# A quarter of a depthwise convolution's taps by ScalarE and adding DMAs, and its layernorm moved into the first MLP matmul

## The chip, the cores and the metric

The kernel runs on one core of a Trainium2 chip. The metric is the device time of one execution in microseconds. Before the change it is 3346.98 us (median of three runs, 3346.12 to 3347.55); the profiled execution spans 3346.6 us with a mean granted TensorE clock of 0.996. All data are float32.

## The reference

The input is eight images of 384 channels and 32 x 32 pixels, that is 1024 tokens of 384 channels. Two layers follow each other.

The first is a transformer block. A layernorm (ln1), q, k and v of 8 heads of 48 channels, softmax attention, a projection (proj) added to the input, a second layernorm (ln2), a linear layer to 1536 channels (fc1) with GELU, a linear layer back to 384 (fc2), added again.

The second is a ConvNeXt block on the first one's output:

```python
y = conv_general_dilated(x, dw_w, padding=((3,3),(3,3)), feature_group_count=384)  # 7x7, one filter per channel
y = layernorm over channels (y + dw_b)                # ln3
y = gelu(y @ w1 + b1)                                 # 384 -> 1536
gx = sqrt(sum over pixels of y**2)
y = gamma * (y * gx / (mean(gx) + eps)) + beta + y    # global response norm
out = x + y @ w2 + b2                                 # 1536 -> 384
```

The depthwise convolution has 49 taps per channel. Nothing is summed over channels in it, so it is not a matmul.

## The kernel before, in words

Channels lie on the 128 partitions: an image is three tiles of 128 channels (index `ct`) by 1024 tokens, and most work goes by halves of 512 tokens. TensorE does the matmuls; fc2, the 384 -> 1536 product of the second block and the 1536 -> 384 product use hand-made fast block multiplications, which trade matmuls for additions on VectorE.

The images overlap by one. In the loop over `b` in `main`, the first layer of image b is computed, and between its parts the second layer of image b-1. In order of TensorE: q and k (`qk`), attention (scores `s`, exp on ScalarE into `p`, products `o`), proj for the first token half, the rest of the attention, fc1 for the first half (`gelu_half`; after its fourth tile `rest` does proj for the second half), fc1 for the second half, fc2 (`by_thirds`), `grn_up` of image b-1 (rows named h), the v matmuls of image b+1, `grn_down` of image b-1 (rows named o_p). The last image goes another way (`mlp_by_halves`, `grn_up_straight`), and its own convolution, in two bands of rows written over the space of the attention's weights (rows named wqkv), has to run before the end.

The convolution (`convolution`, L880) is one instruction per tap and channel tile on VectorE: `acc = window * tap + acc` (L897), 128 x 1024, on a padded copy of the image (`pad`). The 147 instructions of an image are spread over the time of TensorE from the end of `grn_up` to the end of fc1, so that they fill VectorE between its other duties. `Flow` does this spreading: it keeps a planner's clock, which advances by `U` = 0.857 us with each matmul that is written out (`flow.pe`), and side work is a generator that yields the time until its next step is due. A paced chain keeps its own due times. So all queues are in an order fixed when the program is built. `flow.finish` writes out what is left of a chain at once. The second argument of `start_conv` is the time between two taps (1.8 us in the steady images, 1.6 for image 0's convolution, 1.5 for image 6's), the third says for how many rounds of three they are 2.43 us apart.

A layernorm (`layernorm`, L393) takes the sum over channels, subtracts the mean, sums the squares and scales. The sum over partitions is a matmul with a matrix of ones (`token_sums`, L367). Unfolded this is one 128 x 128 matmul of 512 columns per half and sum (L374). Folded, a DMA issued by GpSimd first adds one half of the partitions onto the other (L382), and 64 x 64 matmuls (L388) run side by side in the array. The folded way needs a wait for that DMA, for which the planner leaves 3.4 us. ln1 and the first half of ln2 are folded, the second half of ln2 and ln3 are not. `abreast` runs the two halves of a layernorm together.

ln3 of image b-1 is started by `next_norms`, which `mlp` calls just before fc2: it finishes the convolution's chain, and spawns ln3 followed by `block_differences` (four subtractions that `grn_up` needs). ln1 of image b+1 comes 50 us or more after this.

The attention normalises its products by sums that travel through three small DMAs on SyncE's queue (`average`, L547: sums, back, r), before the multiplication at L579 that proj waits for.

DMAs issued by GpSimd (rows marked POOLq) go out in order of its queue. In fc1 these are the two `difference` DMAs (fc_e, L708) that prepare fc2, in fc2 and `grn_down` the `adding` DMAs (L786).

Of the kernel before, what the change touches and what calls it, by code (L numbers as in the profile page):

```python
# [51 lines left out]
P = 128  # L52
# [12 lines left out]
CM = 2  # L65
NC = HT // CM
U = 0.857
SCALE = HD ** -0.5
EPS0, EPS1, GRN_EPS = 1e-5, 1e-6, 1e-6
SUM_LOW, SUM_HIGH = 1e-25, 1e25  # L70
# [80 lines left out]
def block_kernel(  # L151
# [429 lines left out]
    def attention(b, xt, qT, kT, last_tile, first):  # L581


        sums = two.tile([P, 2 * NP * 8], F32, tag="sums", name=f"sums_{b}")
        outs, chains, ps, backs = {}, {}, {}, ({}, {})

        def scores(qh, m, t):
            s = ps_s.tile([P, 2, NH], F32, tag="s", name=f"s_{b}_{qh}_{m}_{t}")
            for j in range(2):
                for i in range(2):  # L590
                    k0 = t * P + 64 * i
                    nc.tensor.matmul(  # L592
                        out=s[64 * i : 64 * i + 64, j, :],
                        lhsT=kT[64 * j : 64 * j + HD, m, k0 : k0 + 64],
                        rhs=qT[64 * j : 64 * j + HD, m, half(qh)],
                        start=True,
                        stop=True,
                    )
            flow.pe(U)
            p = three.tile([P, 2, NH], F32, tag="p", name=f"p_{b}_{qh}_{m}_{t}")  # L600
            nc.scalar.activation(p, s, AF.Exp)  # L601
            return p

        def product(qh, m, t, p):
            if t == 0:
                for i in range(2):
                    outs[i] = o_tile(f"o_{b}_{qh}_{m}_{i}")
            for i in range(2):
                keys = slice(64 * i, 64 * i + 64)
                for j in range(2):  # L610
                    at = (2 * m + j) * VW
                    nc.tensor.matmul(  # L612
                        out=outs[i][64 * j : 64 * j + 64, :],
                        lhsT=v[keys, t, at : at + 64],
                        rhs=p[keys, j, :],
                        start=(t == 0),
                        stop=(t == KT - 1),
                    )
            flow.pe(U)
            if t == KT - 1:  # L620
                chains[qh, m] = flow.spawn(average(b, qh, m, dict(outs), sums, backs[qh]))

        steps = [(qh, m, t) for qh in range(2) for m in ORDER for t in range(KT)]
        ln_table()
        ln = None
        for n in range(len(steps) + 2):
            if n == 2:
                last_tile()
            if n < len(steps):
                ps[n] = scores(*steps[n])  # L630
            if n >= 2:
                product(*steps[n - 2], ps.pop(n - 2))
            if n - 2 == len(steps) // 2 + 6:
                for chain in first:
                    flow.finish(chain)
                xn = one.tile([P, CT, N], F32, tag="xn", name=f"xn2_{b}")
                for m in (NP - 1, *range(CT)):
                    flow.finish(chains[0, m])
                proj(b, xt, 0)
                slow = 1.4 if b in (1, B - 1) else 1.0  # L640
                ln = layernorm(xt, xn, 0, eps0, "g2", f"ln2_{b}", False, spaced=True, slow=slow, fold="columns")
                ln = flow.spawn(ln)
# [75 lines left out]
    def mlp(b, xt, xn, weights, tag, ln, rest, before_fc2):  # L718

        hid = one.tile([P, HT * N], F32, tag="big", name=f"hid_{b}").rearrange("p (m n) -> p m n", m=HT)  # L720
        e = [three.tile([P, 2, NH], F32, tag="p", name=f"fc2_e_{b}_{i}") for i in range(2)]
        wa = f"fc1_{tag}"
        flow.finish(ln)
        for m in range(HT):
            gelu_half(hid, m, 0, xn, weights, wa, f"fc1_{b}")
            if m == 3 and rest:
                rest()
                slow = 1.2 if b == 1 else 1.0
                ln = flow.spawn(layernorm(xt, xn, 1, eps0, "g2", f"ln2_{b}", True, slow=slow))
        flow.finish(ln)  # L730
# [146 lines left out]
        nc.sync.dma_start(out=kept.rearrange("(c p) n -> p c n", p=P), in_=xt)  # L877
        return kept

    def convolution(acc, us, slow=0, y0=0, y1=H, ready=tuple(range(CT))):  # L880

        done = [0] * CT
        ct, n = None, 0
        while min(done) < KS * KS:
            left = [c for c in ready if done[c] < KS * KS]
            ct = min([c for c in left if c != ct] or left, key=lambda c: done[c])
            i = done[ct]
            dy, dx = divmod(i, KS)  # L890
            window = pad[:, ct, dy + y0 : dy + y1, dx : dx + W]
            dst = image(acc[:, ct, :])[:, y0:y1, :]
            tap = col("dww", ct * KS * KS + i)
            if i == 0:
                nc.vector.tensor_scalar(dst, window, tap, col("dwb", ct), ALU.mult, ALU.add)
            else:
                nc.vector.scalar_tensor_tensor(dst, window, tap, dst, ALU.mult, ALU.add)  # L897
            done[ct] += 1
            n += 1
            yield 2.43 if n <= CT * slow else us  # L900

    def block_differences(acc):

# [76 lines left out]
    def grn_down_straight(b, y, kept, weights, tag, index, todo):  # L980
# [5 lines left out]
        def load():  # L986
            if len(res) < len(todo):
                r, part = todo[len(res)]
                t = three.tile([P, NH], F32, tag="res", name=f"res_{b}_{r}_{part.start}")[:, : part.stop - part.start]
                nc.sync.dma_start(out=t, in_=kept[r * P : (r + 1) * P, part])  # L990
                res.append(t)

# [162 lines left out]
    def prepare(weights, aside):  # L1155
# [23 lines left out]
            return parts  # L1179

        def spare(name):
            return three.tile([P, NH], F32, tag="res", name=name)

        def sub(dst, x, y):
            nc.vector.tensor_tensor(dst, x, y, ALU.subtract)
# [119 lines left out]
    def main():  # L1305
# [41 lines left out]
        state = {"xn": xn, "conv": None, "acc": None, "norm1": None, "norm3": None}  # L1347
        kept = {}

        def start_conv(b, us, slow=0):  # L1350
            state["acc"] = one.tile([P, CT, N], F32, tag="acc", name=f"acc_{b}")
            state["conv"] = flow.spawn(convolution(state["acc"], us, slow), paced=True)

        def next_norms(b, ln=None):
# [28 lines left out]

        def last_convolution(h, ct, ln=None):
            if ct < 0:
                next_norms(B - 1, ln)
                return
            ready[h].append(ct)
            if ct == 0:
# [6 lines left out]
        for b in range(B):  # L1396
# [4 lines left out]
            qT, kT, last_tile = qk(b, state["xn"])  # L1401
            ln2, rest, xn = attention(b, xt, qT, kT, last_tile, (folding, aside) if b == 0 else ())
            if b < B - 1:
                mlp(b, xt, xn, weights, b, ln2, rest, lambda: next_norms(b))
# [58 lines left out]
    def exact_path():  # L1463

        load_wqkv(nc.scalar, nc.scalar)
        with tc.For_i(0, B) as b:
# [11 lines left out]
            mlp("x", xt, xn, weights, "x", ln, None, None)  # L1478
# [111 lines left out]
```

## Time and profile before

| | value |
|---|---|
| time, median of three | 3346.98 us |
| TensorE busy | 3303.6 us, 99% |
| VectorE busy | 2550.6 us, 76% |
| ScalarE busy | 1421.0 us, 42% |
| GpSimd busy | 208.1 us, 6% |
| DMA, mean | 84 GB/s; GpSimd's queue 77.08 MB, 11.9% of 16 engines' span |
| convolution taps, 128 x 1024 | 1008 of 1276 ns |
| period of a steady image | 404.3 us (a row of fc1 at 1346.57 and at 1750.83) |

A row of the costliest groups gives line, engine and operation, what is written and read, shapes and count, then the busy time in us and the mean of one in ns, then the idle time of the engine just before, and what ended it. In the order of time, a row merges equal instructions that follow each other: start, duration, engine, line, and how many. A float32 matmul shows as two records; ends of matmuls are modelled, so the distance of two starts tells what one takes. In a list of DMA issues the last number is the median time from issue to landing.

### The profile page before, as it was taken

What the parts mean: (1) busy time and instruction counts of PE and PEld (TensorE: products, weight loads), DVE (VectorE), ACT (ScalarE), POOL (GpSimd) and SP (SyncE); (2) the same over time, 40 slices, a digit from 0 to 9 for tenths busy, and PEclk for the clock granted to TensorE, in tenths of its full rate; (3) what the DMA queues carried; (4) which work ended last, traced back from release to release, by engine and by line L of the source; (5) the groups of instructions that cost most, each with busy time, mean ns of one, the idle gap of its engine ahead of it and who ended that gap; (6) DMA issues with size and microseconds to landing.
All of it is one profiled execution on the core that took longest, in us unless ns stands there. A gap on an engine that the chain in (4) does not pass through costs nothing.

```text
span 3346.6 us, 37477 instructions
## 1 busy us (share of the span) xinstructions
PE 3303.6 (99%) x14282; PEld 1416.7 (42%) x14282; DVE 2550.6 (76%) x3133; ACT 1421.0 (42%) x1884; POOL 208.1 (6%) x243
## 2 busy tenths in 40 slices
PE   8999999999999999999999999999999999999999
PEld 4344434443344433444334443444434444334455
DVE  4344788887877878779797796967888779989950
ACT  3442453444534354352552625426254353522641
POOL 2121000100000000100001000010000110000000
PEclk9999999999999999999999999999999999999999
DMA  5336102642125410445005350062501633023231
GB/s 185 111 105 148 52 20 57 158 102 63 25 70 146 115 47 20 105 122 135 20 16 131 96 140 17 17 157 80 128 18 37 170 83 95 20 56 90 62 98 50
DMA packets 151243, 281.59 MB, mean 84 GB/s; under 512 B 35216, under 2 KB 41232, under 8 KB 150672
## 3 DMA queue, kind: packets, MB, share of 16 engines
q1 hardware_dynamic: 114704, 201.32, 19.6%
q0 software_dynamic: 36064, 77.08, 11.9%
q8 instruction: 115, 1.88, 0.2%
q10 hardware_dynamic: 288, 0.71, 0.1%
q14 instruction: 72, 0.59, 0.1%
HBM read 181.52 MB, written 33.82 MB: 64 GB/s over the span
## 4 chain that ended last, share of the span: by engine, by line
PE 87%; DVE 10%; DMA 2%; issue 1%; ACT 0%; SPq 0%; POOL 0%; DVEq 0%; POOLq 0%
PE o L612 12%; PE s L592 12%; PE fc L345 12%; PE h L352 10%; PE fc_p L352 10%; PE o_p L352 9%; PE qk L332 6%; DVE wqkv L897 4%; PE v L521 4%; PE o L1000 4%; PE proj L535 3%; DVE acc L897 3%; PE h_last L1044 1%; PE qk_last L345 1%; PE ln_var L374 1%
## 5 line engine op out<-in xcount | busy, mean ns | idle before, releaser
L897 DVE SCALAR_TENSOR_TENSOR acc<-pad,vec,acc 128x1024 f32<-128x1024 f32 x1008 | 1230.6, 1276 | 0.0
L601 ACT ACTIVATE p<-s 128x1024 f32<-128x1024 f32 x512 | 523.6, 1024 | 380.6 <-PE s L592 378.4
L592 PE MATMUL s<-qk 48*64 48x512 f32 x4096 | 544.0, 592 | 1.6 <-ACT qk L495 1.5
L612 PE MATMUL o<-p,v 64*64 64x512 f32 x4096 | 538.9, 590 | 0.0
L345 PE MATMUL fc<-xn,fc 128*128 128x512 f32 x1152 | 500.4, 593 | 0.0
L345 PEld LDWEIGHTS fc<-xn,fc 128*128 128x128 f32 x1152 | 218.2, 190 | 278.2 <-issue 268.2
L352 PE MATMUL fc_p<-hid,fc 128*128 128x512 f32 x728 | 318.1, 592 | 0.0
L364 ACT ACTIVATE hid<-fc,bfc_f 128x512 f32<-128x512 f32 x192 | 130.9, 687 | 357.5 <-PE fc L345 357.4
L612 PEld LDWEIGHTS o<-p,v 64*64 64x64 f32 x4096 | 158.6, 133 | 284.6 <-issue 278.1
L592 PEld LDWEIGHTS s<-qk 48*64 48x64 f32 x4096 | 155.5, 133 | 286.0 <-issue 264.3
L945 DVE TENSOR_TENSOR y<-h,y 128x512 f32<-128x512 f32 x288 | 197.2, 690 | 97.8 <-PE h L352 87.3
L352 PE MATMUL o_p<-y,w 128*128 128x512 f32 x624 | 270.9, 592 | 0.0
L352 PEld LDWEIGHTS fc_p<-hid,fc 128*128 128x128 f32 x728 | 138.2, 190 | 174.4 <-issue 170.4
L332 PE MATMUL qk<-xn,wqkv 128*128 128x512 f32 x480 | 207.4, 592 | 0.0
L352 PE MATMUL h<-acc,w_A 128*128 128x512 f32 x432 | 206.4, 596 | 0.0
L897 DVE SCALAR_TENSOR_TENSOR wqkv<-pad,vec,wqkv 128x416 f32<-128x416 f32 (+1 forms) x288 | 193.7, 749 | 0.6
L352 PEld LDWEIGHTS o_p<-y,w 128*128 128x128 f32 x624 | 118.0, 190 | 148.7 <-issue 133.5
L553 DVE TENSOR_TENSOR attn<-o,attn 128x512 f32<-128x512 f32 x64 | 44.1, 689 | 147.2 <-ACT attn L551 147.2
L495 ACT ACTIVATE qk<-qk,bqk 128x1024 f32<-128x1024 f32 x40 | 44.6, 1114 | 229.0 <-PE qk L332 229.0
L712 ACT COPY pad<-x 128x512 f32<-128x512 f32 x48 | 30.2, 635 | 258.3 <-DVE x L777 192.4
L332 PEld LDWEIGHTS qk<-xn,wqkv 128*128 128x128 f32 x480 | 91.1, 190 | 114.1 <-issue 112.0
L535 PE MATMUL proj<-attn,wproj_sb 128*128 128x512 f32 x288 | 129.2, 602 | 2.1 <-DVE attn L579 2.1
(296 smaller groups left out, 3342.5 us busy)
## 6 DMA issues: line engine op xcount, KB each, us to landing
w_A<-in_w SPq DMA_DIRECT2D x72, 384.0 KB, 3.2
fc<-s_fc SPq DMA_DIRECT2D x91, 256.0 KB, 2.8
hid<-hid POOLq DMA_DIRECT2D x42, 512.0 KB, 6.7
fc<-in_wfc SPq DMA_DIRECT2D x54, 384.0 KB, 5.7
w<-s_w SPq DMA_DIRECT2D x78, 256.0 KB, 2.7
y<-y POOLq DMA_DIRECT2D x36, 512.0 KB, 7.0
kept<-x SPq DMA_DIRECT2D x8, 1536.0 KB, 8.3
xn<-in_x SPq DMA_DIRECT2D x14, 768.0 KB, 7.0
```

What stands on the lines that cost most here:

```text
L332: nc.tensor.matmul(out=ps[:, half(h)], lhsT=lhsT(k), rhs=rhs(k)[:, half(h)], start=(k == 0), stop=(k == nk - 1),)
L345: nc.tensor.matmul(out=ps, lhsT=lhsT(k), rhs=rhs(k)[:, half(h)], start=(k == 0), stop=(k == nk - 1))
L352: nc.tensor.matmul(out=bank, lhsT=lhsT, rhs=rhs, start=k == 0, stop=k == len(pairs) - 1)
L364: nc.scalar.activation(dst, src, function, **kw)
L521: nc.tensor.matmul(out=ps[:, :C], lhsT=xn[:, k, t * P : (t + 1) * P], rhs=wv_sb[:, k, :], start=(k == 0), stop=(k == CT - 1),)
L535: nc.tensor.matmul(out=ps, lhsT=wproj_sb[:, m, ct * P : (ct + 1) * P], rhs=attn[:, m, :], start=(m == 0), stop=(m == CT - 1),)
L592: nc.tensor.matmul(out=s[64 * i : 64 * i + 64, j, :], lhsT=kT[64 * j : 64 * j + HD, m, k0 : k0 + 64], rhs=qT[64 * j : 64 * j + HD, m, half ...
L601: nc.scalar.activation(p, s, AF.Exp)
L612: nc.tensor.matmul(out=outs[i][64 * j : 64 * j + 64, :], lhsT=v[keys, t, at : at + 64], rhs=p[keys, j, :], start=(t == 0), stop=(t == KT - 1),
L897: nc.vector.scalar_tensor_tensor(dst, window, tap, dst, ALU.mult, ALU.add)
L945: nc.vector.tensor_tensor(dst, bank, part, ALU.add)
L1000: nc.tensor.matmul(out=ps, lhsT=tiles[k], rhs=y(k, part), start=(k == 0), stop=(k == HT - 1))
```

## The change

A new chain, `help_convolution`, runs beside the convolution of images 0 to 6. For one channel tile after the other (2, 1, 0) it takes the last 12 of the 49 taps. For each tap and half of the rows ScalarE multiplies the window by the tap into a spare tile (128 x 512, four buffers), and a DMA issued by GpSimd adds this onto `acc`. The steps are 2.4 us apart, with 8 us before each tile and after the last; they pause during `grn_down`. VectorE does the other 37 taps per tile and leaves alone the tile that the helper is at. The time between VectorE's taps becomes 2.05 us (1.75 for image 0's convolution).

The convolution thus ends earlier, near the end of fc1's first half, and ln3 moves from fc2 into fc1: `conv_norm` spawns it behind the second half of ln2, and it is now folded. The purpose is to relieve VectorE and to halve the matmul time of ln3's sums. The factor that stretches the first half of ln2 in images 1 and 7 goes from 1.4 to 1.2.

```diff
+HELPED = 12
-                slow = 1.4 if b in (1, B - 1) else 1.0
+                slow = 1.2 if b in (1, B - 1) else 1.0
...
                 ln = flow.spawn(layernorm(xt, xn, 1, eps0, "g2", f"ln2_{b}", True, slow=slow))
+                behind_ln(ln)
...
-        while min(done) < KS * KS:
-            left = [c for c in ready if done[c] < KS * KS]
+        taps = KS * KS - (HELPED if taken is not None else 0)
+        while min(done) < taps:
+            left = [c for c in ready if done[c] < taps and not (taken and c == taken[-1])]
+            if not left:
+                yield 1.0
+                continue
...
+    def help_convolution(acc, us, taken, paused):
+        yield 8.0
+        for ct in reversed(range(CT)):
+            taken.append(ct)
+            for i in range(KS * KS - HELPED, KS * KS):
+                dy, dx = divmod(i, KS)
+                for h in range(2):
+                    while paused():
+                        yield 2.0
+                    t = three.tile([P, NH], F32, tag="res", bufs=4, name=f"tap_{ct}_{i}_{h}")
+                    y0 = dy + h * H // 2
+                    window = pad[:, ct, y0 : y0 + H // 2, dx : dx + W]
+                    tap = col("dww", ct * KS * KS + i)
+                    nc.scalar.mul(t.rearrange("p (h w) -> p h w", w=W), window, tap)
+                    nc.gpsimd.dma_start(out=acc[:, ct, half(h)], in_=t, accum_op=ALU.add)
+                    yield us
+            yield 8.0
+        taken.append(None)
...
+            state["help"] = flow.spawn(help_convolution(acc, 2.4, taken, paused), paced=True)
+
+        def conv_norm(b, ln):
             if b > 0:
                 acc = state["acc"]
+                norm = abreast(acc, acc, eps1, "lnw", f"ln3_{b - 1}", True)
+                if b < B - 1:
+                    norm = sequence(norm, block_differences(acc))
+                state["norm3"] = flow.spawn(after(ln, after(state["help"], after(state["conv"], norm))))
+
+        def next_norms(b):
+            if b > 0:
+                flow.finish(state["help"])
                 flow.finish(state["conv"])
-                norm = abreast(acc, acc, eps1, "lnw", f"ln3_{b - 1}", True, fold=False)
-                norm = sequence(norm, block_differences(acc)) if b < B - 1 else after(ln, norm)
-                state["norm3"] = flow.spawn(norm)
...
-                start_conv(b, 1.6)
+                start_conv(b, 1.75)
...
-                start_conv(b, 1.5 if b == B - 2 else 1.8, 10)
+                start_conv(b, 2.05, 8)
...
+                state["paused"] = True
                 grn_down(b - 1, y, xt, weights, b - 1, b - 1)
+                state["paused"] = False
```

More of the change, by code (lines that the diff above doesn't have):

```diff
@@ L716, in add_first, with mlp @@
         nc.vector.scalar_tensor_tensor(dst, bank, col("bfc2", r), dst, ALU.add, ALU.add)
-    def mlp(b, xt, xn, weights, tag, ln, rest, before_fc2):
+    def mlp(b, xt, xn, weights, tag, ln, rest, before_fc2=None, behind_ln=None):
         hid = one.tile([P, HT * N], F32, tag="big", name=f"hid_{b}").rearrange("p (m n) -> p m n", m=HT)
@@ L878, in keep, with convolution @@
         return kept
-    def convolution(acc, us, slow=0, y0=0, y1=H, ready=tuple(range(CT))):
+    def convolution(acc, us, slow=0, y0=0, y1=H, ready=tuple(range(CT)), taken=None):
         done = [0] * CT
         ct, n = None, 0
-        while min(done) < KS * KS:
-            left = [c for c in ready if done[c] < KS * KS]
+        taps = KS * KS - (HELPED if taken is not None else 0)
[4 more added lines that the diff above has]
+                continue
             ct = min([c for c in left if c != ct] or left, key=lambda c: done[c])
@@ L988, in load @@
                 r, part = todo[len(res)]
-                t = three.tile([P, NH], F32, tag="res", name=f"res_{b}_{r}_{part.start}")[:, : part.stop - part.start]
+                t = three.tile([P, NH], F32, tag="res", bufs=4, name=f"res_{b}_{r}_{part.start}")[:, : part.stop - part.start]
                 nc.sync.dma_start(out=t, in_=kept[r * P : (r + 1) * P, part])
@@ L1181, in spare @@
         def spare(name):
-            return three.tile([P, NH], F32, tag="res", name=name)
+            return three.tile([P, NH], F32, tag="res", bufs=4, name=name)
         def sub(dst, x, y):
@@ L1345, in main @@
         nc.vector.tensor_scalar(bqk[:, :CT], bqk[:, :CT], SCALE, None, ALU.mult)
-        state = {"xn": xn, "conv": None, "acc": None, "norm1": None, "norm3": None}
+        state = {"paused": False, "help": None, "xn": xn, "conv": None, "acc": None, "norm1": None, "norm3": None}
         kept = {}
         def start_conv(b, us, slow=0):
-            state["acc"] = one.tile([P, CT, N], F32, tag="acc", name=f"acc_{b}")
-            state["conv"] = flow.spawn(convolution(state["acc"], us, slow), paced=True)
-        def next_norms(b, ln=None):
+            acc = state["acc"] = one.tile([P, CT, N], F32, tag="acc", name=f"acc_{b}")
+            taken = []
+            state["conv"] = flow.spawn(convolution(acc, us, slow, taken=taken), paced=True)
+            paused = lambda: state["paused"]
+            state["help"] = flow.spawn(help_convolution(acc, 2.4, taken, paused), paced=True)
+        def conv_norm(b, ln):
             if b > 0:
                 acc = state["acc"]
+                norm = abreast(acc, acc, eps1, "lnw", f"ln3_{b - 1}", True)
[5 more added lines that the diff above has]
+                flow.finish(state["help"])
                 flow.finish(state["conv"])
-                norm = abreast(acc, acc, eps1, "lnw", f"ln3_{b - 1}", True, fold=False)
-                norm = sequence(norm, block_differences(acc)) if b < B - 1 else after(ln, norm)
-                state["norm3"] = flow.spawn(norm)
             if b + 1 < B:
@@ L1385, in last_convolution @@
             if ct < 0:
-                next_norms(B - 1, ln)
+                conv_norm(B - 1, ln)
+                next_norms(B - 1)
                 return
@@ L1403, in main @@
             if b < B - 1:
-                mlp(b, xt, xn, weights, b, ln2, rest, lambda: next_norms(b))
+                mlp(b, xt, xn, weights, b, ln2, rest, lambda: next_norms(b), lambda ln: conv_norm(b, ln))
             else:
@@ L1477, in exact_path @@
             ln = layernorm(xt, xn, 1, eps0, "g2", "ln2_x", True)
-            mlp("x", xt, xn, weights, "x", ln, None, None)
+            mlp("x", xt, xn, weights, "x", ln, None)
             kept = keep("x", xt)
```

## The prediction, made before the changed kernel ran

> **What bounds the kernel now.** I read the page's busy times first, then TensorE's waits by stage, then TensorE's order of time around the layernorms.
>
> ```profile
> PE 3303.6 (99%) x14282; PEld 1416.7 (42%) x14282; DVE 2550.6 (76%) x3133; ACT 1421.0 (42%) x1884; POOL 208.1 (6%) x243
> L897 DVE SCALAR_TENSOR_TENSOR acc<-pad,vec,acc 128x1024 f32<-128x1024 f32 x1008 | 1230.6, 1276 | 0.0
> L601 ACT ACTIVATE p<-s 128x1024 f32<-128x1024 f32 x512 | 523.6, 1024 | 380.6 <-PE s L592 378.4
> ```
>
> TensorE is busy 99% of the span. The convolution is almost half of VectorE's time, yet VectorE has 24% idle, so only where VectorE makes TensorE wait is its relief worth anything. The waits of TensorE, in three windows of the view of who waited for whom (us in total, times, longest): one image of the steady run (1346 to 1751 us), then image 1 (334 to 540), then the last (2782 to the end; its largest two):
>
> ```profile
> PE ln_var L374 <- DVE ln_sq L430: 0.4, 2, 0.2
> PE s L592 <- ACT qk L495: 0.2, 1, 0.2
> ```
> ```profile
> PE proj L535 <- DVE attn L579: 2.1, 1, 2.1
> PE ln_var L388 <- DMA ln_sq<-ln_sq: 1.2, 1, 1.2
> PE ln_var L374 <- DVE ln_sq L430: 0.5, 1, 0.5
> ```
> ```profile
> PE ln_var L374 <- DVE ln_sq L430: 7.3, 2, 5.9
> PE ln_sum L374 <- DVE ln_a L409: 2.4, 1, 2.4
> ```
>
> A steady image (404.3 us from the fc1 row at 1346.57 to that at 1750.83) waits 0.6 us. There only fewer matmuls help. Images 1 and 7 have waits on VectorE.
>
> Next, TensorE's order of time: the sums of the convolution's layernorm (unfolded, in fc2), and those of the next image's (folded).
>
> ```profile
> 1392.06 1.02 PE L374 MATMUL ln_sum<-ln_a,ones 128*128 128x512 f32 x2
> 1392.92 1.02 PE L374 MATMUL ln_sum<-attn,ones 128*128 128x512 f32 x2
> 1393.78 2.74 PE L352 MATMUL fc_p<-hid,fc 128*128 128x512 f32 x6
> ...
> 1449.66 0.65 PE L388 MATMUL ln_sum<-ln_a,ones 64*64 64x512 f32 x2
> ...
> 1450.19 0.62 PE L388 MATMUL ln_sum<-ln,ones 64*64 64x512 f32 x2
> 1450.74 1.12 PE L352 MATMUL h<-acc,w_A 128*128 128x512 f32 x2
> ```
>
> From start to next start: two unfolded sums take 1.72 us (one is 0.86), two folded ones 1.08.
>
> **What the Trainium skill says.** "DMA: Bandwidth & Descriptors", section "Anatomy of one DMA", fits a GpSimd DMA at 2.0 us plus bytes over 436 GB/s: 3.2 us for 512 KB. This trace's adding DMAs of that size take 5.2 us, so the trace is used:
>
> ```profile
> fc_e<-hid POOLq DMA_DIRECT2D x14, 512.0 KB, 5.2
> ln_a<-ln_a POOLq DMA_DIRECT2D x16, 64.0 KB, 2.6
> ln_sq<-ln_sq POOLq DMA_DIRECT2D x7, 128.0 KB, 2.7
> ```
>
> The same page, "Queues, rings and completion order", says that a ring is consumed in order and that an engine takes turns between queues packet by packet. The trace agrees in outline: fc_e, alone in its queue, lands in 5.2 us, while hid<-hid, issued in close pairs, takes 6.7. "TensorE: Matmul & The Clock Gate", Part 1, says that an idle window of about 3.4 us halves the clock. The trace shows a penalty already after 2.1 us: image 1's proj starts at 513.52 and the next fc at 525.29, 11.8 us instead of 18 records of 0.43 us, 7.7; 2.1 is the wait, the rest slow matmuls.
>
> **Removed.** Seven convolutions give up 36 of 147 taps each: 252 x 1.276 us = 322 us of VectorE, 46 per image. In a steady image this hides behind TensorE. In image 1 waits are 4.0 us (2.1, 1.2, 0.5 and 0.2), and the slow clock about 2 more: take 4 saved, bounds 0 and 6. In the last image 2.4 and 0.6 us (layernorm of the attention's output, before the last convolution) can go: take 3. The wait of 5.9 us stays: the last image's own convolution keeps all taps and runs then. Seven layernorms (four 512-column sums each) are folded: 28 x 0.43 = 12.0 us of TensorE by the ideal, 14 pairs x 0.64 = 9.0 by the rows above. Take 10.5.
>
> **Added on ScalarE.** 504 multiplications, 128x512. Nearest rows: the pad copy 0.635 us, a gelu with a column operand 0.687 (L364). "ScalarE: Activation LUTs", "What ACT_TABLE_LOAD costs", gives 280 ns + 0.833 ns per element, 0.71. Take 0.69. In attention an exp of 1.02 us comes each 1.72 us and ScalarE idles 0.70 of it, so one multiplication fits in a gap; with one per 2.4 us about 0.5 us per exp is taken. Behind a late one wait the exp and then the matmuls of o, but two score tiles are in flight. Cost zero, hidden by the matmuls of s and o.
>
> **Added DMAs.** 504 of 256 KB. Landing between 2.7 us (128 KB) and 5.2 (512 KB): take 3.5. Each waits for the previous one of its half (same bytes), due every 4.8 us, and for its multiplication; it keeps up. In the window of fc2 and the first matmul phase (1346 to 1450 us) GpSimd's queue moved 4.46 MB in 26.3% of 16 engines' 104 us, 163 GB/s, so a tap holds all engines for 1.6 us of 2.4. The attention's windows have only 8% DMA share, so there is room. A tile of channels changes hands with 8 us between, more than a landing, so VectorE, whose attention additions queue behind its taps, should not wait.
>
> **The fold of ln2 behind the taps.** GpSimd issues in order. In the changed order one tap stands just ahead of the two fold DMAs of ln2's sum. In the trace of before:
>
> ```profile
> 1679.90 0.69 DVE L409 TENSOR_TENSOR ln_a<-ln_a,x 128x512 f32<-128x512 f32 x1
> 1680.89 1.68 POOL L382 DMA_DIRECT2D ln_a<-ln_a  x2 [133.56 <-DVE ln_a L409]
> 1684.86 0.61 PE L388 MATMUL ln_sum<-ln_a,ones 64*64 64x256 f32 x8
> ```
>
> The two issues overlap in 1.68 us; the second starts by about 1681.5 and at ln_a's 2.6 us lands at 1684.1: slack 0.7. The tap's multiplication stands behind the exp and copy that end at 1680.65, so is done at 1681.3; the folds move about 1 us later, the second lands at 1685.0 alone and up to 1.6 later behind the tap's data. TensorE, and all matmuls of the attention behind it, wait 0.2 to 1.7 us, seven times. Take 0.6: 4 us. The fold of ln2's variance stands at a change of tiles and has slack 1.4 by the same reckoning (issue at 1694.5, matmul at 1699.06): zero.
>
> **ln3 inside fc1.** Its first addition on VectorE waits for the last tap, issued two tiles of fc1 (over 5 us) earlier: no cost. Its variance fold now stands in GpSimd's queue behind the second fc_e DMA (512 KB, 5.2 us). In the changed order TensorE asks for the variance some 7 us after the matmuls of the tile that this fc_e needs. Before its multiplication (1.05 us) ScalarE has a gelu and what is left of six squares (0.63 each): it issues about 2.6 us after those matmuls, lands at 7.8, and the folds behind it in the ring 0.5 and 1 us later. Bounds 0 (if ScalarE is earlier or the fold overtakes) and 2.2 us per image, in six images: take 0.7, 4 us. Table loads stay 71; between fc1's gelus ScalarE idles 1.9 us, which takes the rest.
>
> **The attention's last averages** go through three small DMAs in series. At 1729.38 the last multiplication by r starts and ends at 1730.07; proj's third product is at about 1732.4: slack 2.3. Taps in turn with their packets may add 0 to 3 us; take 2, zero cost.
>
> Sum: 3347 - 10.5 - 4 - 3 + 4 + 4 = 3337.
>
> **Rivals.** (a) All waits stay off TensorE: 12.0 + 6 + 3 saved, 3326. For it: ScalarE's and DMA's idle shares. (b) The new waits give back the gain: 10.5 + 4 saved, 14 returned, 3346. For it: the slacks of 0.7 and 2.3 us are small. (c) Slower: fold waits at 1.3 x 7 = 9, ln3 at 2.2 x 6 = 13 and 4 of slow clock behind these, the averages 0.9 x 7 = 6, against 10.5 + 3 saved: 3365. For it: each new wait meets a TensorE that has no idle time to hide it; against it: VectorE, with a tap every 2.05 us instead of 1.8, does its part of these chains earlier. (d) A tap's landing over 4.8 us makes the buffers bind, multiplications block exps: 0.6 us x 50 taps x 7 = 210, about 3555. Against it: 5.2 us is what twice the size takes.
>
> **How the numbers follow.** Forecast 0.36, (a) 0.18, (b) 0.17, (c) 0.25, (d) 0.04. Faster by over 0.2%: 0.54; within: 0.17; slower: 0.29. The range 3326 to 3362 leaves out (d) and the outer parts of (a) and (c), together under 0.2.
>
> **What would show it.** TensorE's waits in a steady image: on DMA ln_a and DMA ln_sq or attn under 1.5 us in sum. No L374 sum from ln3. Taps landing at 3 to 4.5 us. exp's idle before it down to about 0.2 us. Image period near 404.3 - 1.5 + 1.3 = 404. Image 1's proj with no wait. The forecast is wrong if waits on DMA exceed 2 us per image, if exps wait behind multiplications that wait for a buffer, or if image 7 loses more than before to its last convolution.

## The result: slower by 1.0%, and the profile after

The changed kernel takes 3378.8 us (median of four runs, 3378.0 to 3381.6), the kernel before 3346.6 (median of four). The ratio is 1.0097, interval 1.008 to 1.0115: 32 us slower (27 to 38) where 10 us faster was forecast.

First the page: the busy times, and the group of the new DMAs.

```profile
PE 3317.1 (98%) x14338; PEld 1449.2 (43%) x14338; DVE 2259.2 (67%) x2881; ACT 1723.0 (51%) x2388; POOL 659.1 (20%) x775
L923 POOL DMA_DIRECT2D acc<-tap x504 | 428.3, 856 | 1310.1 <-ACT tap L922 714.4
```

VectorE lost the 291 us that were taken from it (2550.6 to 2259.2), ScalarE took 302 us more, and TensorE's span grew all the same. So VectorE was relieved, and the time went into TensorE's waits. The view of who waited for whom, over the whole span (us in total, times, longest), has these rows which were small or absent before:

```profile
PE proj L536 <- DVE attn L580: 9.7, 7, 3.2
PE ln_var L389 <- ACT hid L365: 3.1, 4, 0.8
PE ln_sum L389 <- DMA ln_a<-ln_a: 3.1, 5, 0.7
```

In the kernel before, proj waited 2.1 us once, a folded sum 0.9 us once, and no ln_var waited for hid. The named waits grew by some 13 us only. To find the rest, compare TensorE's starts: where a matmul record starts later than 0.429 us per 512 columns after the one ahead of it (a quarter for matmuls of 64 columns, which run side by side), the difference is lost. By this count the kernel before loses some 84 us and the changed one 123; 39 more, less the 12 of folded sums, is 27 of the 30 us by which the two profiled spans differ. Most of the losses lie in three places of every image, and they make the distance between the first qk matmuls of two steady images 407.4 to 410.5 us, where it was 404.3 and 404 was forecast.

Part of the loss is clock. After waits of TensorE the clock that the profile records as granted falls to 0.50 for 3.4 or 6.8 us. Without the first 150 us and the last 10 of the program this makes 10 us in the kernel before and 24 in the changed one. At half speed the difference is worth an estimated 7 us of TensorE's time. One such stretch lies in a steady image, from 1799.0 us for 3.4 us, behind the wait of place 1.

A fourth loss stands in the last image alone. From 400 us behind its first qk matmul on, the count gives 8.5 us where it was 3.8. There a residual addition now stands ahead of the squares of the last layernorm in VectorE's queue; TensorE waits 1.8 us for them (ln_var at 3248.51) and the clock falls to 0.50 at 3249.7. The runs below show this wait wherever ln3 of the earlier images is folded, in the kernel before as well, and not where it is unfolded: it is an effect of the fold on the written order, and no DMA stands in that chain.

**Place 1: the variance of ln3, in fc1's second half.** The timeline of one image (start, duration, engine; behind it the idle time before and what ended it):

```profile
1382.60 1.19 POOL L709 DMA_DIRECT2D fc_e<-hid  x1 [4.01 <-ACT fc_e L708]
...
1383.34 1.32 POOL L383 DMA_DIRECT2D ln_sq<-ln_sq  x1
...
1389.09 1.08 PE L389 MATMUL ln_var<-ln_sq,ones 64*64 64x512 f32 x4 [0.80 <-ACT hid L365]
...
1390.19 1.08 PE L389 MATMUL ln_var<-attn,ones 64*64 64x512 f32 x4
...
1391.20 1.99 PE L346 MATMUL fc<-xn,fc 128*128 128x512 f32 x4
```

The fold of ln_sq is issued 0.7 us behind fc_e (512 KB), which lands at 1388.08; ln_sq's lands at 1388.95 and the second one, attn's, at 1390.06, 5.6 and 6.2 us after issue. TensorE starts the first of the two sums (two matmuls side by side, twice) 0.14 us after the first landing, the second 0.13 after the second. The two sums take 2.11 us to the next fc, 1.1 more than undisturbed ones (1.01, in a run below), and by the count of starts the first stands 0.96 us late. The profile names the gelu (hid) because it ended at 1389.02, a moment after the DMA.

**Place 2: the sum of ln2, in the attention.**

```profile
1281.97 0.84 POOL L923 DMA_DIRECT2D acc<-tap  x1 [3.49 <-ACT tap L922]
...
1282.51 2.01 POOL L383 DMA_DIRECT2D ln_a<-ln_a  x2
...
1286.17 0.79 PE L389 MATMUL ln_sum<-ln_a,ones 64*64 64x256 f32 x6 [0.65 <-DMA ln_a<-ln_a]
```

A tap just ahead of the two folds; these land 3.5 and 3.3 us after issue, not 2.6.

**Place 3: proj's second half.** VectorE's timeline at the end of the attention, changed kernel and then the kernel before. L554 (L553) is the last addition of the attention's products, L580 (L579) the multiplication by r; the first L580 shown belongs to the last but one average.

```profile
1321.29 0.69 DVE L580 TENSOR_TENSOR attn<-attn,r 128x512 f32<-128x512 f32 x1 [4.52 <-DMA r<-back]
1321.90 2.48 DVE L903 SCALAR_TENSOR_TENSOR acc<-pad,vec,acc 128x1024 f32<-128x1024 f32 x2
1324.30 0.68 DVE L554 TENSOR_TENSOR attn<-o,attn 128x512 f32<-128x512 f32 x1
...
1333.95 0.69 DVE L580 TENSOR_TENSOR attn<-attn,r 128x512 f32<-128x512 f32 x1 [3.67 <-DMA r<-back]
```
```profile
1717.63 0.69 DVE L579 TENSOR_TENSOR attn<-attn,r 128x512 f32<-128x512 f32 x1 [1.83 <-DMA r<-back]
...
1720.96 0.69 DVE L553 TENSOR_TENSOR attn<-o,attn 128x512 f32<-128x512 f32 x1 [0.24 <-ACT attn L551]
...
1729.38 0.69 DVE L579 TENSOR_TENSOR attn<-attn,r 128x512 f32<-128x512 f32 x1 [0.82 <-DMA r<-back]
```

Before, 8.4 us lie between the last addition and the last multiplication; now 9.65, 1.2 more. But the larger part comes earlier: VectorE stands 4.5 us idle at the head of its queue, waiting for the r of the last but one average, and when that comes, two taps (2.5 us) stand ahead of the last addition. ScalarE had its operand ready at 1322.32 (a copy of 0.59 us from 1321.73); the addition begins 2.0 us later. Together that is 3.2 us, and proj, whose third product needs the last multiplication, starts it 0.6 us late in this image; the longest wait of proj is 3.2 us, in image 1:

```profile
1334.69 6.28 PE L536 MATMUL proj<-attn,wproj_sb 128*128 128x512 f32 x14 [0.47 <-DVE attn L580]
```

What slows places 2 and 3 is in the lists of DMA issues of the two kernels between 350 and 2780 us (KB, median us to landing), before and after:

```profile
r<-back SPq DMA_DIRECT2D x72, 32.0 KB, 2.0
ln_a<-ln_a POOLq DMA_DIRECT2D x12, 64.0 KB, 2.6
```
```profile
acc<-tap POOLq DMA_DIRECT2D x433, 256.0 KB, 3.5
r<-back SPq DMA_DIRECT2D x72, 32.0 KB, 2.9
ln_a<-ln_a POOLq DMA_DIRECT2D x12, 64.0 KB, 3.4
```

The taps land as forecast. But the small DMAs of the attention beside them take longer, those of SyncE's queue too, where no tap stands ahead.

### The profile page after: what moved, and what is told of

It is laid out like the page before. It is cut to its first block, busy times and chain, and to the rows that moved or that the text cites. A ratio compares the mean times of both kernels' runs of the same rounds, so it can differ in the third digit from the quotient of the medians.

```text
span 3376.7 us, 39109 instructions
## 1 busy us (share of the span) xinstructions
PE 3317.1 (98%) x14338; PEld 1449.2 (43%) x14338; DVE 2259.2 (67%) x2881; ACT 1723.0 (51%) x2388; POOL 659.1 (20%) x775
## 4 chain that ended last, share of the span: by engine, by line
PE 69%; DVE 9%; DMA 7%; issue 3%; SPq 1%; ACT 1%; POOL 0%; DVEq 0%; ACTq 0%; POOLq 0%
PE h L353 10%; PE fc L346 10%; PE fc_p L353 10%; PE s L593 8%; PE o_p L353 8%; PE o L613 7%; PE qk L333 4%; PE o L1026 4%; PE v L522 3%; DVE acc L903 3%; DVE wqkv L903 3%; DMA r<-back 2%; PE h_last L1070 2%; DMA sums<-attn 1%; DMA acc<-tap 1%
## 5 line engine op out<-in xcount | busy, mean ns | idle before, releaser
L903 DVE SCALAR_TENSOR_TENSOR acc<-pad,vec,acc 128x1024 f32<-128x1024 f32 x756 | 931.4, 1274 | 1.6
L923 POOL DMA_DIRECT2D acc<-tap x504 | 428.3, 856 | 1310.1 <-ACT tap L922 714.4
L593 PE MATMUL s<-qk 48*64 48x512 f32 x4096 | 586.9, 593 | 2.0 <-ACT qk L496 1.9
L613 PE MATMUL o<-p,v 64*64 64x512 f32 x4096 | 581.4, 590 | 0.0
L922 ACT ACTIVATE tap<-pad,vec 128x512 f32<-128x512 f32 x504 | 359.6, 724 | 56.6 <-DMA acc<-tap 56.4
L613 PEld LDWEIGHTS o<-p,v 64*64 64x64 f32 x4096 | 188.8, 133 | 266.5 <-issue 259.5
L593 PEld LDWEIGHTS s<-qk 48*64 48x64 f32 x4096 | 183.7, 133 | 270.3 <-issue 209.2
L554 DVE TENSOR_TENSOR attn<-o,attn 128x512 f32<-128x512 f32 x64 | 44.0, 687 | 163.9 <-ACT attn L552 163.9
```

What stands on the lines that cost most here:

```text
L593: nc.tensor.matmul(out=s[64 * i : 64 * i + 64, j, :], lhsT=kT[64 * j : 64 * j + HD, m, k0 : k0 + 64], rhs=qT[64 * j : 64 * j + HD, m, half ...
L613: nc.tensor.matmul(out=outs[i][64 * j : 64 * j + 64, :], lhsT=v[keys, t, at : at + 64], rhs=p[keys, j, :], start=(t == 0), stop=(t == KT - 1),
L922: nc.scalar.mul(t.rearrange("p (h w) -> p h w", w=W), window, tap)
L923: nc.gpsimd.dma_start(out=acc[:, ct, half(h)], in_=t, accum_op=ALU.add)
```

## The experiments

My theory (1) was: the tap DMAs, and the large DMA ahead of ln3's fold, hold up the three small DMA chains that TensorE waits for. Rivals: (2) ScalarE's multiplications delay the chains; (3) the fold of ln3 is the main loss in itself. All results first, each as the difference to the kernel before, from the ratio's interval times 3347 us. The runs were made on several chips, each beside the kernel before, so that two of them are compared by their ratios; such a difference of two, called a gain below, is uncertain by about 8 us:

| run | difference, us | interval |
|---|---|---|
| the changed kernel | +32 | 27 to 38 |
| without tap DMAs | +3 | 0 to 6 |
| without tap DMAs and multiplications | 0 | -3 to 3 |
| ln3 not folded | +29 | 23 to 35 |
| kernel before, ln3 folded in fc2 | +20 | 14 to 25 |
| fc_e behind the folds | +16 | 10 to 22 |
| no taps around ln2's sum | +20 | 13 to 26 |
| no taps around the last averages | +17 | 11 to 22 |
| earlier averages' products later | +21 | 15 to 27 |
| paused in two windows, step 2.0 us | +56 | 49 to 64 |
| three mends | -8 | -11 to -5 |
| one tile helped | -6 | -8 to -3 |
| no taps moved | +12 | 7 to 17 |

**Without the tap DMAs.**

```diff
                     nc.scalar.mul(t.rearrange("p (h w) -> p h w", w=W), window, tap)
-                    nc.gpsimd.dma_start(out=acc[:, ct, half(h)], in_=t, accum_op=ALU.add)
```

> The changed kernel with its 504 adding DMAs of the taps left out (the last 12 taps of each channel tile are missing from the convolutions of images 0 to 6); ScalarE's 504 multiplications stay. Theory 1 (the tap DMAs hold up the small DMA chains that TensorE waits for: ln2's sum fold, about 1.3 us in seven images; the attention's averages, about 13 us in all with the slow clock behind them; and 0.5 us behind the late proj in six images): those about 22 us come back and the wait on ln3's variance fold (about 2.2 us in six images) stays: 3357 us, landing of r and attn back to 2.0 us. Theory 2 (ScalarE's multiplications delay the copies, squares and exps of these chains): the DMAs are not to blame, 3374 or more. Theory 3 (ln3's fold inside fc1 is the main loss): 3372 or more.

Measured: 3352.1 us against 3348.8 for the kernel before on the same chip, so 29 us of the 32 come back (expected: 22). The steady period is 404.8 or 404.9 us in four of five images. No row of proj is left among TensorE's waits; that of ln_var on hid is, at 3.9 us. The row of ln_sum on ln_a is back to the 0.9 us of the kernel before. So the tap DMAs are the cause of nearly all of the 32 us: theory 1 stands as far as the taps go, theory 2 falls.

**Without the helper.** The multiplication goes too.

```diff
-                    t = three.tile([P, NH], F32, tag="res", bufs=4, name=f"tap_{ct}_{i}_{h}")
-                    nc.scalar.mul(t.rearrange("p (h w) -> p h w", w=W), window, tap)
-                    nc.gpsimd.dma_start(out=acc[:, ct, half(h)], in_=t, accum_op=ALU.add)
```

> As the run without the tap DMAs, and the 504 multiplications of ScalarE are left out too (the same taps are missing). Theory 1: within 2 us of that run, 3357 us. Theory 2: the time falls only here, to about 3355 from 3374. Theory 3: 3372 or more here as well.

Measured: 3347.3 us. Against the run above it is 0.8 per thousand (2.7 us) less, with intervals that overlap: ScalarE's multiplications cost little or nothing. What is left, a fold of 12 us by the ideal and VectorE's relief, brings no gain at all. Place 1, worth 16 us in a run below, and the wait in the last image are large enough to eat it; that was not tried without the helper.

**ln3 unfolded, in fc1.**

```diff
-                norm = abreast(acc, acc, eps1, "lnw", f"ln3_{b - 1}", True)
+                norm = abreast(acc, acc, eps1, "lnw", f"ln3_{b - 1}", True, fold=False)
```

> The changed kernel with ln3 of images 0 to 6 not folded but still inside fc1. Theory 1: the wait on its variance fold (2.2 us in six images, 13 us) goes and four halves of matmuls come back in seven images (9 to 12 us): 3373 to 3378. Theory 3 (ln3's fold is the main loss, with what follows from it in the slow clock): 3360 or less.

Measured: 3377.5 us, as theory 1 has it. Theory 3, which said 3360 or less, falls for this kernel: with the fold or without it the time is the same. It is no clean balance of the fold alone, for in this run's profile proj waits 18.6 us in all, 9.7 in the changed kernel; why is open.

**Only the fold, in the kernel before.**

```diff
-                norm = abreast(acc, acc, eps1, "lnw", f"ln3_{b - 1}", True, fold=False)
+                norm = abreast(acc, acc, eps1, "lnw", f"ln3_{b - 1}", True)
```

> The kernel before, with one change: ln3 of images 0 to 6 is folded where it was, in fc2. Theory 1 (a fold loses only where its DMAs wait behind others): fc2's own adding DMAs of 512 KB take 6.7 us to land in the same queue, so part of the 9 to 12 us is given back: 3338 to 3347. Theory 3 (the fold as such costs more than it saves): 3350 or more.

Measured: 3367.1 us, a miss for my expectation of 3338 to 3347. There the fold's DMA is issued beside fc2's adding DMAs of 512 KB and lands after 3.1 us; ln_var waits 8.7 us in all (2.2 before), 1.1 per image. And the longer chain moves ln3's last VectorE instructions, so that they stand ahead of a block addition of fc2, at about the same loss:

```profile
1848.79 2.39 PE L352 MATMUL fc_p<-hid,fc 128*128 128x512 f32 x5 [1.07 <-issue]
```

The profile names no releaser, but VectorE's addition into hid (L777) ends at 1848.69, 0.1 us before, with six multiplications of ln3 and the first differences ahead of it in the queue; that this order is the cause is read from the trace, not tried. The wait in the last image is here too. So fc2, as it is written, was a bad place for the fold.

**fc_e behind the folds.**

```diff
-            if m in (3, 5):
-                two_tiles = hid[:, m - 3 : m - 1, :]
-                difference(e[(m - 3) // 2], ...)
+            if m in (7, 9):
+                i = m // 2 - 3
+                two_tiles = hid[:, 2 * i : 2 * i + 2, :]
+                difference(e[i], ...)
```

> The changed kernel with the two fc_e DMAs behind tiles 7 and 9 of fc1's second half instead of 3 and 5, so that the folds of ln3's variance stand ahead of them in GpSimd's queue. Theory 1a (the folds land late because they stand behind 512 KB in the queue): about 2.2 us of waits and slow clock come back in six images, 3379 - 13 = 3366, and the folds land in about 2.7 us instead of 5 to 6. Theory 1b (the wait is for the bank that the gelu before it frees, which the profile names): the row of that wait stays at 0.8 us per image and the time at 3375 or more.

Measured: 3365.1 us, 16 us better by the ratios. The folds of 128 KB land after 2.8 us (ln_sq) instead of 4.1, and the two sums of ln3's variance run through:

```profile
1384.46 0.65 PE L389 MATMUL ln_var<-ln_sq,ones 64*64 64x512 f32 x2
...
1385.47 7.99 PE L346 MATMUL fc<-xn,fc 128*128 128x512 f32 x18
```

1.01 us to the next fc, 2.11 in the changed kernel. The row of ln_var on hid is gone: the DMA was the cause, the gelu only the name. Against the unfolded run the time is 13 us less, near the fold's 12 of the ideal; but the waits of proj differ between these two runs as well (10.5 and 18.6 us), so it is no measure of the fold.

**No taps around ln2's sum.** A flag is up from proj's first half to the matmuls of ln2's first sum (the chain's third step lowers it); while it is, the DMA is not issued and its tap is missing.

```diff
-                    nc.gpsimd.dma_start(out=acc[:, ct, half(h)], in_=t, accum_op=ALU.add)
+                    if not quiet[0]:
+                        nc.gpsimd.dma_start(out=acc[:, ct, half(h)], in_=t, accum_op=ALU.add)
...
+                quiet[0] = True
                 proj(b, xt, 0)
...
-                ln = flow.spawn(ln)
+                ln = flow.spawn(speaking(ln, 2))
```

> The changed kernel without the 42 tap DMAs (six in each of images 1 to 7) that are issued between proj's first half and the matmuls of ln2's first folded sum; their multiplications stay, the taps are missing from the result. Theory 1 (a tap just ahead delays the fold): its DMAs land in 2.6 us again and 1.1 us per image comes back, 3379 - 8 = 3371. Rival (the fold was late for VectorE's order, not for the DMA): no more than 2 us.

Measured: 3367.7 us, 13 us better by the ratios (expected 8); ln_a of 64 KB lands after 2.5 us, and its row of waits falls from 3.1 to 0.7 us.

**No taps around the last averages.** The same flag, up from the last product of a half until proj.

```diff
+            if n - 2 == len(steps) // 2 - 1 or n - 2 == len(steps) - 1:
+                quiet[0] = True
...
+                quiet[0] = False
                 proj(b, xt, 0)
...
+            quiet[0] = False
             proj(b, xt, 1)
```

> The changed kernel without the 66 tap DMAs that are issued while the attention's last averages of each half travel through their three small DMAs (from the last product of the half to proj); their multiplications stay, the taps are missing from the result. Theory 1 (the averages are slowed by taps in another queue, through the shared DMA engines): r lands in 2.0 us there again, proj no longer waits, 10 us of waits and 6 of slow clock and of the late sum behind it come back, 3379 - 16 = 3363. Rival (proj is late because VectorE and ScalarE are): no more than 4 us.

Measured: 3368.0 us, 16 us better by the ratios, as expected. proj waits 2.6 us in all, 9.7 in the changed kernel.

**The earlier averages' products later.** This asks how the taps reach proj, with all of them in place.

```diff
-        yield 2.4
+        yield 2.4 if m == 2 else 6.0
         nc.vector.tensor_tensor(attn[:, m, :], attn[:, m, :], r, ALU.mult)
```

> The changed kernel with one number altered: in the attention's averages the multiplication by r of all but the last one is written out 6.0 instead of 2.4 us after its DMAs, so that on VectorE it stands behind the last addition of the half and not ahead of it. All tap DMAs stay. Theory 1c (the slowed r DMA of the last but one average holds VectorE, idle for 4.5 us in the trace, and the last addition queues behind it; some 2 of proj's 2.9 us of delay come this way): proj's waits fall from 9.7 us to 3 or less, 3379 - 10 = 3369. Rival (the last average's own three DMAs, each slowed, make proj late): no more than 3 us, 3376 or more.

Measured: 3368.3 us, 11 us better, as expected; no row of proj is left, though r still lands after 3.1 us. VectorE in the same place as above:

```profile
1319.88 0.69 DVE L554 TENSOR_TENSOR attn<-o,attn 128x512 f32<-128x512 f32 x1 [3.02 <-ACT attn L552]
1320.48 0.68 DVE L580 TENSOR_TENSOR attn<-attn,r 128x512 f32<-128x512 f32 x1
```

The addition comes as soon as ScalarE's copy is there, and the multiplication, whose r has long landed, costs nothing behind it. So the slow DMA harmed proj through VectorE's order: with the DMAs as slow and the order changed, proj's 9.7 us of waits are gone.

**Paused in two windows.** A first attempt at a better version: both windows above, really paused, with ten taps per tile and a step of 2.0 us; fc_e stands behind the folds.

```diff
-                    while paused():
+                    while paused() or quiet[0]:
...
-            state["help"] = flow.spawn(help_convolution(acc, 2.4, taken, paused), paced=True)
+            state["help"] = flow.spawn(help_convolution(acc, 2.0, taken, paused), paced=True)
```

> A whole version: the helper takes 10 taps per tile instead of 12, a step every 2.0 us, pauses in both of these windows, VectorE's taps every 1.95 us, and the fc_e DMAs stand behind the folds of ln3's variance. Nothing is left out. Theory 1 (three places, additive): 3379 - 13 - 8 - 16 = 3342. Rival (the pauses only move the taps' harm to other places, for example the first averages, qk's DMAs or the last part of fc1's first half): 3358 or more.

Measured: 3404.6 us; the rival of this run holds. TensorE waits 26.5 us for ScalarE's copies of qk, eight times, up to 5.0. ScalarE's timeline in one image:

```profile
1615.08 0.74 ACT L933 ACTIVATE tap<-pad,vec 128x512 f32<-128x512 f32 x1 [0.79 <-DMA acc<-tap]
1615.73 1.10 ACT L497 ACTIVATE qk<-qk,bqk 128x1024 f32<-128x1024 f32 x1
```

Ahead of this, the next image's input (1.5 MB) is loaded in 9 us, and a tap issued at 1599.04 lands at 1606.96, 7.9 us after issue. At a step of 2.0 us the four buffers are full, the multiplication waits for one, and the copy of qk waits behind it in ScalarE's queue. It is the prediction's rival (d), in a small place. In the changed kernel, with 2.4 us, the same load is there (landings up to 9.8 us), but ScalarE catches up in time: s waits 1.9 us for qk in all, 1.5 before. Step and pauses were changed together here; the version below, with one of the pauses and a step of 2.4 us, has no such wait (1.6 us).

**Three mends.** fc_e behind the folds, the later products, and a pause around ln2's sum only, with 11 taps per tile at 2.4 us and VectorE's taps at 2.0 us.

```diff
-HELPED = 12
+HELPED = 11
-                    while paused():
+                    while paused() or quiet[0]:
```

> A whole version, nothing left out: the changed kernel with the fc_e DMAs behind tiles 7 and 9, the late multiplications of the averages, and a helper that pauses from proj's first half until ln2's first folded sum, with 11 taps per tile instead of 12 to make up for it (VectorE's taps every 2.0 us). The pace stays at 2.4 us, so that qk's part of the image is as in the changed kernel. Theory 1: 3379 - 14 - 10 - 9 = 3346, level with the kernel before. Rival (the waits move on, as in the version paused in two windows): 3360 or more.

Measured: 3339.4 us against 3347.1, ratio 0.9976 (0.9968 to 0.9985): faster than both kernels. Against the changed kernel that is 40 us (34 to 47). The three single gains, 16, 13 and 11 us, add up to 40 as well; each of them is uncertain by 8 us, so the close agreement is luck, but that the gains add up, roughly, is shown. My expectation, with 14, 9 and 10, was 3346. The steady period is 403.6 to 404.9 us, and ln_a and ln_sq of 64 KB land after 2.6 us.

**One tile helped.** The helper does one channel tile only, early in the attention. VectorE does the other 135 taps.

```diff
+HELPED_TILES = (2,)
...
-        for ct in reversed(range(CT)):
+        for ct in HELPED_TILES:
...
-                start_conv(b, 2.05, 8)
+                start_conv(b, 1.7, 8)
```

> A whole version: the helper does 12 taps of the last channel tile alone (24 steps of 2.4 us, over early in the attention), VectorE the other 135, one every 1.70 us, so that the convolution still ends where ln3 can start in fc1; the fc_e DMAs stand behind tiles 7 and 9. Theory 1 (late taps' DMAs cost, VectorE's time hardly does): no waits on ln2's fold and proj from taps, 12 us of matmuls saved: 3335 to 3340, faster than before. Rival (VectorE, 10% denser in the attention, now makes proj and ln2 late itself): 3350 or more.

Measured: 3342.3 us, ratio 0.9983 (0.9975 to 0.9991), also faster, by less than expected; against the run above the intervals overlap. In the steady image from 1165 to 1572 us no DMA wait of ln2 and none of proj is left, and r lands after 2.0 us again.

**No taps moved.** VectorE does all taps, faster; fc_e stands behind the folds here and in the run above.

```diff
-HELPED = 12
+HELPED = 0
...
-            state["help"] = flow.spawn(help_convolution(acc, 2.4, taken, paused), paced=True)
+            taken.append(None)
...
-                start_conv(b, 2.05, 8)
+                start_conv(b, 1.55, 8)
```

> A whole version without any helper: VectorE does all 147 taps, one every 1.55 us (1.55 in image 0's convolution as well), ln3 folded inside fc1, the fc_e DMAs behind tiles 7 and 9. Theory 1: DMAs as in the kernel before, 12 us of matmuls saved, and some waits on VectorE as in image 1 of the kernel before (2 us of proj in each image and as much of slow clock): 3340 to 3360. Rival (VectorE is not short at all, its relief was never needed): 3337 or less.

Measured: 3361.3 us, 1 us above the range that I expected: VectorE was short, and at this pace, the only one tried, ln3 in fc1 does not pay without a helper. The rows that are larger than in the changed kernel are on VectorE: ln_var on ln_sq 9.3 us in all (3.0 there), qk on an addition of the second block (kept) 4.0 (none there).

## Why the prediction was wrong

The sum was 3347 - 17.5 saved + 8 of new waits. The savings came out somewhat smaller (8 us are left with the three mends; 13 by the run without tap DMAs, less the 16 us of place 1); the new waits are 40 us or more. The step that failed is the pricing of these waits: one chain was put at nothing, two were mis-sized.

- **The attention's averages, "take 2, zero cost": wrong, and the largest miss in kind.** I followed only the last average, from r's landing to proj, and found a slack of 2.3 us. Its own three DMAs lengthened by 1.2 us in the rows above, less than the 2 that I took. What was not in it is the average ahead of it: slowed as well, it holds VectorE at the head of its queue and pushes the last addition back by 2.0 us. Together that is more than the slack. The late products won 11 us, no taps there 16, against the forecast's zero.
- **The fold of ln3, "take 0.7, bounds 0 and 2.2": the mechanism was right, the size wrong.** The folds stand behind the second fc_e, as written, which landed about when I had it. But they landed 0.9 and 2.0 us behind it, not 0.5 and 1, and each had its own wait: 2.1 us in the image above (0.96 and 1.1), near my upper bound. By the times it is 16 us in six images, 2.7 each (1.4 to 4).
- **The fold of ln2, "take 0.6, bounds 0.2 to 1.7": mechanism right, mis-sized.** The two landed at 1286.03 and 1286.39, 3.5 and 3.3 us after issue where 2.6 was the figure before. By the times seven images cost 13 us, 1.9 each (0.6 to 3); by the count of starts the attention of a steady image loses 1.3 us more than before, inside the bounds and twice what I took.
- **Folded sums, 10.5 saved: about right** where nothing waits: two undisturbed sums take 1.01 us to the next matmul where two unfolded ones took 1.72, 0.7 us for each of 14 pairs, 10 us. But I counted a gain that depended on place 1, and the fold brought the wait in the last image, which I had put at nothing; that this image would lose more was one of the signs against the forecast, and it did (25 us by the count of starts, 21 before).
- **VectorE's relief: right, but spent again.** Without taps' DMAs proj no longer waits in image 1. With them it waits 3.2 us there, more than the 2.1 before, against the forecast's "no wait". In image 7 the wait of 2.4 us on ln_a is gone as forecast, but ln2's folded variance waits 1.6 us for its DMA (0.6 before).
- **ScalarE at zero: right.** A multiplication takes 0.724 us (estimate 0.69), exp's idle time for s falls from 378 to 198 us in all (0.4 us each, where 0.2 was forecast), and s waits hardly more.
- **Tap landing 3.5 us, and rival (d) at 0.04: right** for the changed kernel.

Rival (c), slower, was the case that came, with just these three waits; it said 3365, with the averages at 6 us and all three somewhat too small. What it had for it, "each new wait meets a TensorE that has no idle time", was the argument to weigh higher. The slow clock, which it counted with 4 us, is in the trace as well, some 7 us over the whole span, but not behind every wait: at 1334.69, after proj's wait of 0.5 us, 14 records take 6.1 us to the next row, as at full speed.

One of the signs was badly chosen. Waits on DMA above 2 us per image were to show that the forecast is wrong; by the rows of named waits a steady image has 1.5 at the most (the one named after the gelu counted in), and only the starts of the matmuls show that the two folds cost more than 3.

"DMA: Bandwidth & Descriptors", section "Queues, rings and completion order", in the Trainium skill, says that a ring is consumed in order (it says so of the rings that SyncE and ScalarE use) and that an engine serves its queues in turn, packet by packet. The runs agree with both: ln3's ln_sq of 128 KB lands after 5.6 us behind fc_e in GpSimd's queue and after 2.9 ahead of it (one image of each trace), and r in SyncE's queue, which has no tap ahead of it, still goes from 2.0 to 2.9 us. I used the first for the folds and allowed 0 to 3 us for the second, and then chose the value that still fitted into the slack.

Open: how much of the 3.4 us of ln2's fold is the queue and how much the shared engines was not taken apart. The smaller factor for ln2 in images 1 and 7 (1.2 for 1.4), a part of the change, was not tried alone. Nor was it tried whether the three mends together with fewer taps would gain more.

## What to carry to other kernels

Before giving spare DMA capacity to bulk work, list every small DMA that the busiest engine waits for, and ask of each what stands ahead of it in its queue and what shares the engines with it; a small mean utilisation (8% in the attention here) says nothing about these. Follow a slowed chain through the in-order queue of the engine that waits for it: what stands behind the waiting instruction is late too, and writing the waiting one out later was the whole remedy for proj. Give a case in which several small slacks are used up at once more weight than I did. And when sums of named waits do not explain a time, compare the starts of the busiest engine's instructions.

## What the runs showed of the hardware

- Small DMAs beside a stream of 256 KB each 2.4 us took 0.8 to 1.6 us longer (medians): r 2.0 to 2.9 and qk (64 KB) 2.3 to 3.9 in SyncE's queue, ln_a 2.6 to 3.4 in GpSimd's own.
- An adding DMA of 256 KB landed after 3.2 us at the least; beside a load of 1.5 MB it took up to 9.8. One of 512 KB ahead in the same queue made two folds of 128 KB land after 5.6 and 6.2 us; issued ahead of it they took 2.9 and 3.1.
- The granted clock fell to 0.50 for 3.4 us at 1799.0 in the changed kernel, where the longest wait of TensorE in the 10 us before was 0.9 us; after other waits of that size (0.8 us at 1389) it did not.
- Waits in three places of an image added up: mended one by one they gave 16, 13 and 11 us, each uncertain by 8, and together 40 (34 to 47).
